# Rewriting a selective-scan vision block: states on partitions, products shared between VectorE and GpSimd, image stages laid between the scans

## The chip, the cores and the metric

The kernel runs on one core of a Trainium2 chip. The metric is the device time of one execution in microseconds, the median of several runs. Every time below is from the profile of one execution of the kernel before, or from its three timed runs. PE stands for TensorE, DVE for VectorE, ACT for ScalarE, POOL for GpSimd, SP for SyncE.

## What is computed

Input x is four images of 64 x 64 pixels with 96 channels in f32. Layer 0 normalizes x by groups and uses only its sign:

```
xz   = s_in * (sign(gn(x)) @ sign(W_in - mean).T) + b_in   # 96 -> 384, halves xp and z
t    = conv3x3(sign(xp + move0), csc * sign(conv_W))       # 192 -> 192
u    = silu(prelu(t + bias) + rp_b1 + xp)                  # [192, 4096] per image
for k in 4 scans:   # rows, columns, rows backwards, columns backwards
    B, C [16, 4096] and 6 further rows = sign products of u's flat data
    delta = softplus(sign product of the signs of those 6 rows + dt_bias)  # [192, 4096]
    h[d,n,l] = exp(delta[d,l] * A[d,n]) * h[d,n,l-1] + delta[d,l] * u[d,l] * B[n,l]
    y[d,l]   = sum_n h[d,n,l] * C[n,l] + D[d] * u[d,l]
y    = layernorm_channels(y of the 4 scans, turned back and added)
x1   = x + s_out * (sign(y * silu(z)) @ sign(W_out).T) + b_out
```

Layer 1 is an attention without softmax over the 4096 tokens (so q (k^T v) is a product with one 96 x 96 matrix per image), and then a feed-forward 96 -> 384 -> 96 whose factors are rounded to 8-bit floats and whose sums are rounded to 16 bits, each behind a layer norm and added to its input.

The bulk is the recurrence: 4 images x 4 scans x 192 channels x 16 states x 4096 steps.

## The kernel before

**Tiling.** Two images form a pair. The pair's 2 x 192 channels fill three tiles of 128 partitions (T = 0, 1, 2). A scan instruction runs along the free axis over 1024 steps of one state n of 128 channels, so there are 2 pairs x 3 tiles x 4 scans x 4 chunks x 16 states = 1536 scan instructions of 128 x 1024.

**Stages of a pair, one after the other** (`layer0_pair`): signs of the normalized x (L248 to L259), in-projection (L276, L277), convolution as 18 products for each 512 pixels (L297, L300) with the activation chain L308 to L319, projections to B, C and the 6 rows (L350 to L376), the scans, and then layer norm, gate and out-projection (L522 to L566). Layer 1 (`layer1`) follows after both pairs. Nothing of one pair's image stages runs beside the other pair's scans.

**The scans' inner loop**, once per state n (`nm` numbers the tiles):

```python
bp = spread("bp", n)              # L474: PE copies row n of B to all 128 partitions, in PSUM
cp = spread("cp", NS + n)         # the same for C
dA = sw.tile([128, CH], F32, name=f"dA_{nm}", tag="dA")
nc.scalar.activation(dA, delta[:, cols], AF.Exp, scale=c["an"][:, KIND[T], k, n : n + 1])
dB = sw.tile([128, CH], F32, name=f"dB_{nm}", tag="dB", bufs=3)
nc.vector.tensor_tensor(dB, du, bp, ALU.mult)
h = sw.tile([128, CH], F32, name=f"h_{nm}", tag="h")
nc.vector.tensor_tensor_scan(h, dA, dB, 0.0 if ci == 0 else carry[:, n : n + 1], ALU.mult, ALU.add)
if ci < NCH - 1:
    nc.gpsimd.tensor_copy(carry[:, n : n + 1], h[:, CH - 1 : CH])
nc.vector.tensor_tensor(dB, h, cp, ALU.mult)
for j in range(2):
    nc.tensor.matmul(
        y[:, 512 * j : 512 * j + 512], ident, dB[:, 512 * j : 512 * j + 512],
        start=(n == 0), stop=(n == NS - 1),
    )
```

In the profile these are L486 (the decay `dA` on ACT), L488 (`dB`), L490 (the scan), L494 (the carry on POOL), L495 (times C) and L497 (PE sums over n by a product with the identity, into `yp`). VectorE has three passes over 128 x 1024 for each of the 1536 pieces. `prepare` (L414 to L431) makes `delta` for the next job in the middle of a job. The order on each engine is that of the program; a tile framework adds the waits.

Of the kernel before, what the change touches and what calls it, by code (L numbers as in the profile page):

```python
# [1 line left out]

# [24 lines left out]
HID = 384  # L27

# Columns of the per-channel parameters.
# [4 lines left out]
# The 192 inner channels of a pair of images fill three tiles of 128 partitions:  # L34
#   0: channels 0..127 of the first image     1: the same of the second
#   2: channels 128..191 of the first on partitions 0..63, of the second on 64..127
# A parameter column comes in two kinds, for tiles 0 and 1 and for tile 2.
KIND = (0, 0, 1)
# [3 lines left out]
def hybrid_kernel(ctx: ExitStack, tc: tile.TileContext, a: dict, out: bass.AP):  # L42
    nc = tc.nc
    const = ctx.enter_context(tc.tile_pool(name="const", bufs=1))
    dram = ctx.enter_context(tc.tile_pool(name="dram", bufs=1, space=DRAM))
# [4 lines left out]
    def load(name, shape, src=None):  # L50
        t = ctile(name, shape)
        nc.sync.dma_start(t, a[name] if src is None else src)
        return t

    # ------------------------------------------------------------------ constants
    ident = ctile("ident", [128, 128])
    make_identity(nc, ident)
    identb = ctile("identb", [128, 128], BF16)
    nc.vector.tensor_copy(identb, ident)
    ones1 = ctile("ones1", [128, 1])  # L60
# [3 lines left out]
    grp = load("grp", [DM, DM])  # L64
    lnm = load("lnm", [128, 6, 128])
    hmask = load("hmask", [DM, DM])

    pv = load("pv", [128, 2, NPV])
    an = load("al", [128, 2, NK, NS])
    nc.scalar.activation(an, an, AF.Exp)  # L70
    nc.vector.tensor_scalar(an, an, -1.0, None, ALU.mult)
    cbias = ctile("cbias", [128, 2])
    nc.vector.tensor_tensor(cbias, pv[:, :, CONV_B], pv[:, :, RP0], ALU.add)
    dbias = ctile("dbias", [128, 2, NK])
    nc.vector.tensor_tensor(dbias, pv[:, :, BD : BD + NK], pv[:, :, DTB : DTB + NK], ALU.add)
    dsum = ctile("dsum", [128, 2])
    nc.vector.tensor_reduce(dsum, pv[:, :, DSK : DSK + NK], AX.X, ALU.add)

    winT = ctile("winT", [DM, 2 * DN], BF16)
    woutT = ctile("woutT", [128, 2, DM], BF16)  # L80
    cw0 = ctile("cw0", [128, 9, DN], BF16)
    cw1 = ctile("cw1", [128, 9, DN], BF16)
    csc = ctile("csc", [128, 2])
    wlT_bc = ctile("wlT_bc", [64, 3, 128], BF16)
    wlT_dt = ctile("wlT_dt", [64, 3, 128], BF16)
    selw = ctile("selw", [99, 128], BF16)
    sld = ctile("sld", [128, 2])
    wdz = ctile("wdz", [48, NK, 8, DN], BF16)
    so_bc = ctile("so_bc", [128, DM])
    nc.sync.dma_start(so_bc, a["s_out"].partition_broadcast(128))  # L90
    bo_bc = ctile("bo_bc", [128, DM])
    nc.sync.dma_start(bo_bc, a["b_out"].partition_broadcast(128))
    rbs = [ctile(f"rb{i}", [99, CH], BF16) for i in range(4)]
    for t in rbs:
        nc.vector.memset(t[96:99, :], 1.0)

    x1d = dram.tile([NB, L, DM], F32, name="x1d", tag="x1d")
    sgd = dram.tile([NB, NK, NR * L], BF16, name="sgd", tag="sgd")

    # ------------------------------------------------------------------ weights  # L100
    with tc.tile_pool(name="prep", bufs=1) as prep, tc.tile_pool(
        name="prep_ps", bufs=2, space=PSUM
    ) as pps:

        def negmean(name, src, n):
            m = prep.tile([src.shape[0]] + list(src.shape[1:-1]) + ([1] if len(src.shape) == 2 else []), F32, name=name)
            nc.vector.tensor_reduce(m, src, AX.X, ALU.add)
            nc.vector.tensor_scalar(m, m, -1.0 / n, None, ALU.mult)
            return m

        def transposed(dst, src):
            """dst[j, i] = src[i, j], for signs"""
            p, f = src.shape
            ps = pps.tile([128, 128], BF16, name="tps", tag="tps")
            nc.tensor.transpose(ps[:f, :p], src, identb[:p, :p])
            nc.vector.tensor_copy(dst, ps[:f, :p])

        wi = prep.tile([128, 3, DM], F32, name="wi")
        nc.sync.dma_start(wi, a["w_in"].rearrange("(t p) j -> p t j", p=128))
        wim = negmean("wim", wi, DM)  # L120
        wis = prep.tile([128, 3, DM], BF16, name="wis")
        for t in range(3):
            nc.scalar.activation(wis[:, t, :], wi[:, t, :], AF.Sign, bias=wim[:, t : t + 1])
            transposed(winT[:, 128 * t : 128 * t + 128], wis[:, t, :])

        wo = prep.tile([DM, DN], F32, name="wo")
        nc.sync.dma_start(wo, a["w_out"])
        wom = negmean("wom", wo, DN)
        wos = prep.tile([DM, 2, 128], BF16, name="wos")
        nc.scalar.activation(wos[:, 0, :], wo[:, 0:128], AF.Sign, bias=wom)  # L130
        for j in range(2):
            nc.scalar.activation(wos[:, 1, 64 * j : 64 * j + 64], wo[:, 128:192], AF.Sign, bias=wom)
        for j in range(2):
            transposed(woutT[:, j, :], wos[:, j, :])

        for j, dst in ((0, cw0), (1, cw1)):
            cwf = prep.tile([128, 9, DN], F32, name="cwf", tag="cwf", bufs=2)
            nc.sync.dma_start(cwf, a["cw_t"][:, j])
            nc.scalar.activation(dst, cwf, AF.Sign)
            cwn = prep.tile([128, 9 * DN], F32, name="cwn", tag="cwn", bufs=2)  # L140
            nc.sync.dma_start(cwn, a["cw_n"][:, j])
            nc.vector.tensor_reduce(csc[:, j : j + 1], cwn, AX.X, ALU.add, apply_absolute_value=True)
        nc.vector.tensor_scalar(csc, csc, 1.0 / (9 * DN), None, ALU.mult)

        wl = prep.tile([128, DN], F32, name="wl")
        nc.sync.dma_start(wl, a["wl_bc"])
        wld = prep.tile([128, DN], F32, name="wld")
        nc.vector.memset(wld, 0.0)
        nc.vector.memset(sld, 0.0)
        for k in range(NK):  # L150
            nc.sync.dma_start(wld[32 * k : 32 * k + NR, :], a["wl_dt"][k])
            nc.sync.dma_start(sld[32 * k : 32 * k + NR, :], a["sl_dt"][k])
        for src, dst, nm in ((wl, wlT_bc, "b"), (wld, wlT_dt, "d")):
            m = negmean("wlm" + nm, src, DN)
            s = prep.tile([128, DN], BF16, name="wls" + nm)
            nc.scalar.activation(s, src, AF.Sign, bias=m)
            for j in range(3):
                transposed(dst[:, j, :], s[:, 64 * j : 64 * j + 64])

        # B and C rows are sl * (an integer of at most 8 bits) + bl.  One bf16 product  # L160
        # copies such a row to all partitions without loss: sl and bl in three bf16
        # parts each, the integers three times and three rows of ones.
        def parts(name, src):
            got = []
            rest = src
            for j in range(3):
                p = prep.tile(list(src.shape), BF16, name=f"{name}p{j}")
                nc.vector.tensor_copy(p, rest)
                got.append(p)
                if j < 2:  # L170
                    r = prep.tile(list(src.shape), F32, name=f"{name}r{j}")
                    nc.vector.tensor_tensor(r, rest, p, ALU.subtract)
                    rest = r
            return got

        slr = prep.tile([96, NK], F32, name="slr")
        nc.sync.dma_start(slr, a["sl_bc"])
        blr = prep.tile([1, 128], F32, name="blr")
        nc.sync.dma_start(blr, a["bl_bc"])
        for j, p in enumerate(parts("sl", slr)):  # L180
            rows = slice(32 * j, 32 * j + 32)
            pf = prep.tile([96, NK], F32, name=f"slf{j}")
            nc.vector.tensor_copy(pf, p)
            for k in range(NK):
                nc.vector.tensor_scalar(
                    selw[rows, 32 * k : 32 * k + 32], ident[rows, rows], pf[rows, k : k + 1], None, ALU.mult
                )
        for j, p in enumerate(parts("bl", blr)):
            nc.sync.dma_start(selw[96 + j : 97 + j, :], p)

        # wdz[(s, c), k, s', d] = sign of Wd[k, d, c] for s == s', 0 elsewhere
        for j, (d0, dn) in enumerate(((0, 128), (128, 64))):
            wd = prep.tile([dn, NK, NR], F32, name=f"wd{j}")
# [585 lines left out]
```

## Time and profile before

| what | value |
|---|---|
| time, median of 3 runs | 9687.55 us (9681.52 to 9706.05) |
| span of the profiled execution | 9661.7 us |
| VectorE busy | 8266.2 us |
| PE busy | 6867.1 us |
| ScalarE busy | 3015.5 us |
| GpSimd busy | 526.9 us |
| PE's mean granted clock | 0.865 |

A row of the groups gives the line, engine, operation, output and input tiles, shapes, count, then busy time and mean length in ns of one, then the idle time in front of them and the instruction that ended it. The slices cut the span into 40 equal parts of 241.5 us and give the busy share in tenths. In the timeline a row begins with the start and the length in us. In the windows each engine has its busy time within a stretch and, in brackets, how many instructions; then come the granted PE clock as a share of full speed, the DMA engines' busy share and the rate moved.

### The profile page before, as it was taken

What the parts mean: (1) busy time and instruction counts of PE and PEld (TensorE: products, weight loads), DVE (VectorE), ACT (ScalarE), POOL (GpSimd) and SP (SyncE); (2) the same over time, 40 slices, a digit from 0 to 9 for tenths busy, and PEclk for the clock granted to TensorE, in tenths of its full rate; (3) what the DMA queues carried; (4) which work ended last, traced back from release to release, by engine and by line L of the source; (5) the groups of instructions that cost most, each with busy time, mean ns of one, the idle gap of its engine ahead of it and who ended that gap; (6) DMA issues with size and microseconds to landing.
All of it is one profiled execution on the core that took longest, in us unless ns stands there. A gap on an engine that the chain in (4) does not pass through costs nothing.

```text
span 9661.7 us, 55915 instructions
## 1 busy us (share of the span) xinstructions
PE 6867.1 (71%) x20931; PEld 2540.6 (26%) x20931; DVE 8266.2 (86%) x6014; ACT 3015.5 (31%) x2906; POOL 526.9 (5%) x1266
## 2 busy tenths in 40 slices
PE   8976666666676776767897666666666677676766
PEld 2232222222222222222324222222222222222244
DVE  2159999999999999998314999999999999999967
ACT  3143333333333333322314333333333333332223
POOL 0000000000000000000000000000000000000012
PEclk6589999999888989999558999998999899999976
DMA  1000000000000000000100000000000000000011
GB/s 39 7 7 3 3 3 4 3 3 3 3 3 3 4 5 5 5 5 15 29 9 7 3 3 3 3 3 3 3 3 3 3 4 5 5 6 7 12 43 27
DMA packets 110605, 73.14 MB, mean 8 GB/s; under 512 B 95076, under 2 KB 95774, under 8 KB 110238
## 3 DMA queue, kind: packets, MB, share of 16 engines
q1 hardware_dynamic: 110334, 69.58, 2.9%
q8 instruction: 164, 2.69, 0.1%
q14 instruction: 107, 0.88, 0.0%
HBM read 24.71 MB, written 13.37 MB: 4 GB/s over the span
## 4 chain that ended last, share of the span: by engine, by line
DVE 58%; PE 22%; issue 16%; ACT 2%; DMA 1%; SPq 0%; POOL 0%; DVEq 0%; POOLq 0%; ACTq 0%
DVE h L490 32%; DVE dB L488 16%; PE yp L497 8%; DVE dB L495 5%; PE cvps L297 3%; PE cvps L300 3%; DVE y L510 1%; PE bp L474 1%; DVE sd L541 1%; PE mu L522 1%; PE tp L350 1%; PE bc L359 1%; PE dt L364 1%; ACT xr L353 1%; PE at L674 0%
## 5 line engine op out<-in xcount | busy, mean ns | idle before, releaser
L497 PE MATMUL yp<-dB,ident 128*128 128x512 f32 x6144 | 3511.3, 700 | 1404.9 <-DVE dB L495 1401.3
L486 ACT ACTIVATE dA<-delta,al 128x1024 f32<-128x1024 f32 x1536 | 1762.8, 1148 | 4794.9 <-DVE h L490 4752.9
L490 DVE TENSOR_TENSOR_SCAN h<-dA,carry,dB 128x1024 f32<-128x1024 f32 x1152 | 2702.0, 2345 | 37.0 <-DVE dB L488 1.9
L497 PEld LDWEIGHTS yp<-dB,ident 128*128 128x128 f32 x6144 | 1170.5, 211 | 3055.9 <-DVE dB L495 1866.4
L488 DVE TENSOR_TENSOR dB<-du,bp 128x1024 f32<-128x1024 f32 x1536 | 1845.5, 1202 | 140.1 <-PE bp L474 139.2
L495 DVE TENSOR_TENSOR dB<-h,cp 128x1024 f32<-128x1024 f32 x1536 | 1862.0, 1212 | 13.3 <-PE cp L474 3.9
L474 PE MATMUL bp<-rb,selw 99*128 99x512 bf16 (+1 forms) x4096 | 1021.2, 412 | 908.9 <-DVE dB L488 885.0
L474 PEld LDWEIGHTS <-selw 99*128 99x128 bf16 (+1 forms) x8192 | 638.7, 109 | 2683.7 <-issue 2493.2
L474 PE MATMUL cp<-rb,selw 99*128 99x512 bf16 (+1 forms) x4096 | 997.3, 404 | 28.3 <-DVE dB L488 16.5
L490 DVE TENSOR_TENSOR_SCAN h<-dA,dB 128x1024 f32<-128x1024 f32 x384 | 876.9, 2284 | 11.0
L494 POOL COPY carry<-h 128x1 f32<-128x1 f32 x1152 | 406.1, 353 | 8208.9 <-DVE h L490 8208.7
L312 DVE TENSOR_SCALAR t<-t,pv 128x512 f32<-128x512 f32 x48 | 23.3, 486 | 610.5 <-ACT t L308 610.5
L297 PE MATMUL cvps<-tp,cw 128*128 128x512 bf16 (+1 forms) x576 | 358.1, 622 | 2.5 <-ACT u L276 2.5
L300 PE MATMUL cvps<-tp,cw 64*128 64x512 bf16 (+1 forms) x576 | 356.4, 619 | 0.0
L427 ACT ACTIVATE sp<-dps,dbias,pv 128x1024 f32<-128x1024 f32 x96 | 115.5, 1203 | 486.3 <-PE dps L414 285.6
L355 DVE COPY xr<-tp 64x1536 bf16<-64x1536 bf16 x64 | 60.8, 950 | 232.0 <-PE tp L350 232.0
L431 DVE TENSOR_TENSOR delta<-sp,sr 128x1024 f32<-128x1024 f32 x96 | 183.3, 1909 | 46.5 <-ACT sp L430 46.5
L308 ACT ACTIVATE t<-cvps,cbias,csc 128x512 f32<-128x512 f32 x48 | 37.3, 777 | 443.4 <-PE cvps L300 443.4
L350 PE MATMUL tp<-identb,xg 128*64 128x128 bf16 x1536 | 157.5, 259 | 15.1 <-DMA xg<-sg 13.2
L541 DVE RECIPROCAL sd<-sd 128x512 f32<-128x512 f32 x48 | 158.6, 3332 | 10.6 <-ACT sd L540 8.4
L522 PE MATMUL mu<-y,lnm 128*128 128x512 f32 x224 | 130.0, 721 | 45.7 <-DVE yc L532 44.6
L350 PEld LDWEIGHTS <-xg 128*64 128x64 bf16 x1536 | 138.3, 160 | 70.9 <-issue 70.9
(181 smaller groups left out, 3702.9 us busy)
## 6 DMA issues: line engine op xcount, KB each, us to landing
rb<-ibc SPq DMA_DIRECT2D x384, 64.0 KB
xt<-in_x SPq DMA_DIRECT2D x16, 384.0 KB
xr<-in_x SPq DMA_DIRECT2D x32, 192.0 KB
x1d<-o SPq DMA_DIRECT2D x32, 192.0 KB
x<-x1d SPq DMA_DIRECT2D x16, 384.0 KB
out<-o SPq DMA_DIRECT2D x32, 192.0 KB
xg<-sg SPq DMA_DIRECT2D x16, 172.0 KB
cwf<-in_cw_t SPq DMA_DIRECT2D x2, 864.0 KB
```

What stands on the lines that cost most here:

```text
L297: nc.tensor.matmul(ps[prow, :], c["cw0"][:, t, co], tpad[j][:, win[0], win[1]], start=(t == 0), stop=False)
L300: nc.tensor.matmul(ps[prow, :], c["cw1"][rows, t, co], tpad[2][rows, win[0], win[1]], start=False, stop=(t == 8),)
L350: nc.tensor.transpose(tp[:, j // 6, 128 * (j % 6) : 128 * (j % 6) + 128], src, identb)
L474: nc.tensor.matmul(ps[rows, 512 * h : 512 * h + 512], w.to_broadcast([99, rows.stop - rows.start]), t[:, 512 * h : 512 * h + 512], start=True,
L486: nc.scalar.activation(dA, delta[:, cols], AF.Exp, scale=c["an"][:, KIND[T], k, n : n + 1])
L488: nc.vector.tensor_tensor(dB, du, bp, ALU.mult)
L490: nc.vector.tensor_tensor_scan(h, dA, dB, 0.0 if ci == 0 else carry[:, n : n + 1], ALU.mult, ALU.add)
L494: nc.gpsimd.tensor_copy(carry[:, n : n + 1], h[:, CH - 1 : CH])
L495: nc.vector.tensor_tensor(dB, h, cp, ALU.mult)
L497: nc.tensor.matmul(y[:, 512 * j : 512 * j + 512], ident, dB[:, 512 * j : 512 * j + 512], start=(n == 0), stop=(n == NS - 1),)
L522: nc.tensor.matmul(ps, c["lnm"][:, m, :], src[s], start=(i == 0), stop=(i == len(terms[T]) - 1))
L541: nc.vector.reciprocal(sd, sd)
```

## The change

The kernel is rewritten around the same arithmetic. Six things are new.

1. **A piece** is 32 channels x 4 states on 128 partitions, 1024 steps: again 1536 pieces, each with one scan. B and C are stored in DRAM and loaded spread over the 32 channels; delta and delta times u are stored and loaded spread over the 4 states. The sum over 4 states is a PE product with a 0/1 matrix (`sum4`) that adds four partitions, accumulated over four pieces.
2. **Shares.** GpSimd makes the injected product of every piece (`inject`). The product by C goes to VectorE or to GpSimd by a tally of assumed costs, kept while the program is built (`Tally`, `scan`). The decay is written to PSUM.
3. **Order.** One loop over all 1536 pieces (`Scans.run`) writes the order by hand: injected products four pieces ahead, the decay one ahead, the sum over states three behind, stores some rounds after their producers. In each round one step of the image stages of other images is taken (`next(back, None)`): the prologue of images 1 to 3 and the epilogue of images 0 to 2 stand between scans, and most of the last image's norm. Only image 0's prologue (head) and the last image's end (tail) stand alone.
4. **u also stored turned**: beside `ud` (rows) there is `utd` (columns), so that the column scans load whole rows. Their outputs are turned back in a stage of its own (`turn`).
5. **Sign products on the whole array or in bf16**: the projections and delta's products use 128 rows or columns of the array, signs are in 8-bit floats, delta's weights are padded with zeros; u's projection chain is in bf16.
6. **Head and tail**: where an image stands alone, VectorE takes a part of ScalarE's work in the convolution (`v`), the norm and the feed-forward, and in the tail two more lanes work on blocks of 512 pixels side by side. All activations come from one table set (silu, softplus and roots by Exp and Ln).

The core of the diff:

```diff
-                    bp = spread("bp", n)
-                    cp = spread("cp", NS + n)
...
-                    nc.scalar.activation(dA, delta[:, cols], AF.Exp, scale=c["an"][:, KIND[T], k, n : n + 1])
...
-                    nc.vector.tensor_tensor(dB, du, bp, ALU.mult)
...
-                    nc.vector.tensor_tensor(dB, h, cp, ALU.mult)
...
+    def load_bc(self, w, to, b, e, ci, q):
+        c = self.c
+        t = c.p.bc.tile([128, CH], F32, name=f"bc{w}_{b}_{e}_{ci}_{q}", tag=f"bc{w}")
+        src = c.bcd[b][KORD[e], 16 * w + 4 * q : 16 * w + 4 * q + 4, CH * ci : CH * ci + CH]
+        c.nc.sync.dma_start(t, src.unsqueeze(0).to_broadcast([32, 4, CH]))
+        to[b, e, ci, q] = t
...
+            src = c.dld[KORD[e]][b][w, 32 * g : 32 * g + 32, CH * ci : CH * ci + CH]
+            c.nc.sync.dma_start(t, src.unsqueeze(1).to_broadcast([32, 4, CH]))
...
+    def decay(self, i):
...
+        t = c.p.dA.tile([128, CH], F32, name=f"dA_{i}", tag="dA")
+        c.nc.scalar.activation(t, self.dlt[i // NQ][0], AF.Exp, scale=c.anm[:, g, NQ * KORD[e] + q : NQ * KORD[e] + q + 1])
...
+    def inject(self, i):
...
+        t = c.p.w.tile([128, CH], F32, name=f"w_{i}", tag="w")
+        c.gps.tensor_tensor(t, self.dlt[i // NQ][1], self.bt[b, e, ci, q], ALU.mult)
...
+        lead = c.vec.us - c.gps.us
+        c.vec.us, c.gps.us = max(0.0, min(lead, 8.0)), max(0.0, min(-lead, 8.0))
+        pool = c.vec.us + 1.2 > c.gps.us + 2.4
+        dA, w, cr = self.dAs[i], self.ins[i], self.ct[b, e, ci, q]
+        h = c.p.h.tile([128, CH], F32, name=f"h_{i}", tag="h") if pool else dA
+        c.vec.tensor_tensor_scan(h, dA, w, first, ALU.mult, ALU.add)
+        (c.gps if pool else c.vec).tensor_tensor(w, h, cr, ALU.mult)
...
+        for x in range(4):
+            c.nc.tensor.matmul(
+                y[32 * x : 32 * x + 32, g % 2, :], c.sum4, prod[:, 256 * x : 256 * x + 256],
+                start=(q == 0), stop=(q == NQ - 1), tile_position=(0, 32 * x),
+            )
...
+        for i in range(n):
+            self.at = i
+            self.loads(i)
+            if i >= 1:
+                self.carry(i - 1)
+            if i + 1 < n:
+                self.decay(i + 1)
+            full = i % 8 == 3 and i > 8
+            if full:
+                self.evacuate(i - 4)
+            elif i >= 3:
+                self.reduce(i - 3)
+            if i + AHEAD < n:
+                self.inject(i + AHEAD)
+            self.scan(i)
+            c.later.tick()
...
+            interleave(lanes)
+            next(back, None)
```

`c.vec` and `c.gps` are VectorE and GpSimd with the tally; `prepare` in `lanes` makes delta for the chunk after next, one part for every eight pieces; `carry` copies the last column of h on ScalarE.

## The prediction

> **What bounds the kernel now.** I read the page first (busy shares, slices, groups), then the timeline of 12 us inside the scans, then the windows by stage. The page says which engine is full and with what:
>
> ```profile
> span 9661.7 us, 55915 instructions
> PE 6867.1 (71%) x20931; PEld 2540.6 (26%) x20931; DVE 8266.2 (86%) x6014; ACT 3015.5 (31%) x2906; POOL 526.9 (5%) x1266
> ...
> DVE  2159999999999999998314999999999999999967
> ...
> L486 ACT ACTIVATE dA<-delta,al 128x1024 f32<-128x1024 f32 x1536 | 1762.8, 1148 | 4794.9 <-DVE h L490 4752.9
> L490 DVE TENSOR_TENSOR_SCAN h<-dA,carry,dB 128x1024 f32<-128x1024 f32 x1152 | 2702.0, 2345 | 37.0 <-DVE dB L488 1.9
> L488 DVE TENSOR_TENSOR dB<-du,bp 128x1024 f32<-128x1024 f32 x1536 | 1845.5, 1202 | 140.1 <-PE bp L474 139.2
> L495 DVE TENSOR_TENSOR dB<-h,cp 128x1024 f32<-128x1024 f32 x1536 | 1862.0, 1212 | 13.3 <-PE cp L474 3.9
> ```
>
> VectorE is at 9 tenths wherever there are scans, hardly waits (37, 140 and 13 us), and ScalarE waits 4753 us for it. GpSimd does 5%. The timeline, VectorE alone (start, length, instruction), gives the pace:
>
> ```profile
> 3001.20 2.34 DVE L490 TENSOR_TENSOR_SCAN h<-dA,carry,dB 128x1024 f32<-128x1024 f32 x1
> 3003.46 1.19 DVE L488 TENSOR_TENSOR dB<-du,bp 128x1024 f32<-128x1024 f32 x1
> 3004.57 1.21 DVE L495 TENSOR_TENSOR dB<-h,cp 128x1024 f32<-128x1024 f32 x1
> 3005.70 2.34 DVE L490 TENSOR_TENSOR_SCAN h<-dA,carry,dB 128x1024 f32<-128x1024 f32 x1
> ```
>
> From start to start: 2.26 for the scan, 1.11 and 1.13 for the products, 4.50 us a piece; 1536 pieces make 6912 us. The windows (length, busy time of PE, PEld, DVE, ACT and POOL, clock, DMA share, GB/s) show that the rest is image work with VectorE idle, and what DMA can do:
>
> ```profile
> 0.00:483.00 483.00, 423.62 (x1211) 136.81 (x1212) 93.25 (x233) 120.68 (x174) 14.41 (x11) 0.62 0.08 23
> ...
> 900.00:2700.00 1800.00, 1226.99 (x2942) 433.88 (x2942) 1751.99 (x1153) 568.49 (x498) 93.82 (x265) 0.91 0.01 3
> ...
> 100.00:330.00 230.00, 227.46 (x419) 45.83 (x418) 36.68 (x57) 46.61 (x72) 0.00 (x0) 0.50 0.03 9
> ...
> 10.00:15.00 5.00, 0.24 (x1) 0.09 (x1) 1.38 (x3) 1.64 (x1) 0.00 (x0) 1.00 0.99 406
> ```
>
> The first pair of images takes 483 us before its first scan (230 us of it PE alone, the convolution at a granted clock of 0.50); the second pair some 530 more, in which no scan runs. In the scans VectorE works 1752 of 1800 us.
>
> **What the Trainium skill says.** (1) "GPSIMD Engine Reference", section 3.1: a product of two f32 inputs of 2048 elements takes 4497 ns there, about twice VectorE's. The trace of before has no two-input operation on GpSimd; its one-input cast of 512 elements has a median of 668 ns, which agrees with twice that for two inputs. (2) "SBUF — State Buffer", section "Who interferes with whom": a VectorE instruction with two SBUF inputs excludes a GpSimd instruction that reads SBUF; one with a single SBUF input does not. Nothing in before shows it, since GpSimd is idle. (3) "ScalarE: Activation LUTs", "What ACT_TABLE_LOAD costs": an activation without pointer operands takes 186 ns + 0.833 ns per element; with the 93 ns that the section gives for one pointer, 1024 elements come to 1132 ns, and the trace has 1148.
>
> **The change, part by part.**
>
> *The piece.* There are again 1536 scans of 128x1024, now 32 channels by 4 states. Of VectorE's three passes the first (u times delta times B) goes to GpSimd for every piece, and the last (times C) is shared out by a tally as the program is built: counting the program's instructions, 905 stay on VectorE and 631 go to GpSimd. B, C, delta and delta times u no longer come from PE; DMA loads them spread over partitions. The decay exp(delta A) is written to PSUM, so that a scan has one SBUF input (the injected product) and a product by C one (C) where VectorE makes it; by (2) these leave GpSimd free.
>
> *VectorE in the scan stage.* 1536 scans x 2.26 = 3471 us. 905 products x 1.13 = 1023. Preparing delta: 192 parts x 2 operations of 512; such rows of before take 663 and 678 ns, 0.60 by the overlap of 0.08 to 0.1 seen above: 230. Convolution of three images: 48 x 3 x 0.62 = 89. Norm, attention and feed-forward that stand between scans: 28 norm blocks with 4 operations of 512 and 24 feed-forward blocks with 2, 160 x 0.6 = 96, and 28 small ones at 0.25 = 7. Sum 4916 us.
>
> *GpSimd.* 1536 + 631 = 2167 products of 1024. The halved price is 2.25 us; the start-up is not halved, so up to 2.35; I take 2.3: 4984 us. From below: 2.1 us if the second input costs less than the first.
>
> So two engines end up nearly equal, at 3.20 and 3.24 us a piece. Neither hides the other: the tally alternates between both, four injected pieces ahead is all the slack.
>
> *ScalarE.* 1536 decays x 1.15 = 1766; 1152 carry copies at the price of (3), 0.19 = 219; 192 evacuations at 0.59 (row of the 128x512 cast) = 113; 960 operations of delta and about 1700 of the image stages, of 512 elements, at 0.68 (rows of before lie between 0.59 and 0.81) = 1810. Together 3.9 ms, 3.7 of them beside the scans: 70% of the stage. It is hidden on the mean, but it is in order: carry copy i-1 waits for scan i-1, and behind it stand decay i+1 and all image work.
>
> *PE.* The sum over states is four f32 products of 256 columns a piece. In before's timeline four of 512 columns take 1.98 us; half of that is 1.0 us a piece, 1.5 ms in all. Image stages add 1.0 to 1.7 ms by clock. Hidden: 50 to 62%.
>
> *DMA.* 1280 spread loads of 512 KiB = 671 MB. In 5.2 ms that is 129 GB/s, against 406 in the window above. u stored turned makes the loads of the column scans whole rows; its stores are in 128-byte pieces, 6144 a store, 12 beside scans. With the 384-byte rows of x1d moving at 261 GB/s in before (1.5 MB, 4096 pieces, 6 us) such a store takes about 9 us, and the loads are issued 13 to 17 us ahead. I cost it at nothing.
>
> *Head.* Only image 0 stands before the scans, and of its sign projections only two scans of four. Load, sums, turning: 27 us; in-projection 32 activations x 0.75 = 24; convolution 288 products at the 0.54 us from start to start that the clock of 0.50 gives in before = 156, with 16 more of the recomputed projection 165, the last part's chain 12; projection of two scans a quarter of the pair's 153 us window, 40, plus its stores and loads through DRAM 25; first delta parts and spread loads 17. VectorE's share of the convolution lies under PE and costs nothing. Sum 310 us.
>
> *Tail.* Of the 32 norm blocks (8 an image) 28 stand beside scans in the program's order; 4 of the last image are left, and its 8 feed-forward blocks. By the chain of a block's operations at the rows above, a norm block takes some 28 us and a feed-forward block 20. Two rounds of three lanes at 28 us, 8 us for the last y to go through DRAM, 9 for the small matrices; three rounds of 20 us and 3 us of store. Sum 136 us. VectorE's share shortens ScalarE's queue there; the round is a chain, so I take no more from it.
>
> *Sum.* The scan stage has 4984 us of work on its fuller engine. In before VectorE idles 2.7% of its scan stage with every other engine at 70% or less; here two engines are full and two more at 60 to 70% in order, so I take double, 5.3%: 5248. With 310 and 136: **5694 us**.
>
> **Rivals.** *In-order ScalarE and PE set the pace* (6250 us). The convolution's steps put six products (1.5 to 3.3 us) and up to three activations (2 us) plus a delta step (1.4 us) into one piece's time; decay and carry behind them come late, with about 1.9 us of slack. If half of the pieces took 4.3 us (a convolution step of 3.3 us and the sum's 1.0 on PE) and the others 3.24: 1536 x 3.78 = 5800, + 446. For it: the ScalarE share, the 0.50 clock; against: means of 70 and 62%. *GpSimd is quicker than priced* (5500): 2.1 us leaves VectorE the bound, 4916 + 3% + 446. *DMA sets the pace* (6550): 671 MB at 110 GB/s; the same lines are read 32 or 4 times; against: 406 GB/s. *The two engines exclude each other* (10346, slower than before): if the scan counts as two SBUF inputs by its carry, 4984 + 4916 + 446. For it: 1152 scans do read a carry from SBUF beside the product; against: (2) speaks of tensors, and the carry is one element.
>
> **How the numbers follow.** Main case 0.55, ScalarE and PE 0.25, GpSimd quicker 0.12, DMA 0.05, exclusion 0.03. Range: below, VectorE's 4916 without a stall and a head and tail of 420: 5330. Above, the ScalarE and PE case with 6% of stalls more: 6350. Outside stand DMA, exclusion and edges of the others, 0.15 to 0.2. Only exclusion ends above 9687: faster 0.96, same 0.01, slower 0.03.
>
> **What would show it.** Right: the page has GpSimd and VectorE both above 85%; the group of injected products has a mean of 2.2 to 2.4 us, the scans 2.3; VectorE's slices are at 8 or 9 from the third to the last but one; from start to start of a scan 3.2 to 3.5 us; the first scan starts near 310, the last ends near 136 before the end. Wrong: injected products or scans far longer than these (exclusion); waits of VectorE on the decay of several hundred us (ScalarE); waits on spread loads (DMA); a head of 400 us and more, if the convolution in 8-bit runs slower than 0.54 us a product or if the one-byte strided sign writes, like the 1608 ns of before's strided sign row, hold ScalarE.

## The result and the profile after

The changed kernel takes 5776.87 us (median of 4 runs, 5769.06 to 5794.46), against 9696.8 us for the kernel before, run beside it: a ratio of 0.596, 95% interval 0.5946 to 0.5973. Forecast were 5694 us, within 5330 to 6350.

The page of the kernel after, with the lines that answer to those of before:

```profile
span 5775.5 us, 61921 instructions
PE 3419.4 (59%) x19813; PEld 1339.9 (23%) x19813; DVE 5176.7 (90%) x3422; ACT 3672.1 (64%) x5620; POOL 5080.7 (88%) x2291
...
DVE  3299999999889999999999999999999999999984
...
POOL 2099999999889999999998999999999999999980
...
L386 POOL TENSOR_TENSOR w<-dl,bc 128x1024 f32<-128x1024 f32 x1536 | 3578.4, 2354 | 149.2 <-PE yp L1264 73.8
L1223 ACT ACTIVATE dA<-dl,anm 128x1024 f32<-128x1024 f32 x1536 | 1714.0, 1116 | 494.6 <-DVE w L386 254.6
...
L386 DVE TENSOR_TENSOR_SCAN dA<-dA,cy,w 128x1024 f32<-128x1024 f32 x680 | 1593.1, 2343 | 109.7 <-ACT dA L1223 94.0
L386 POOL TENSOR_TENSOR w<-h,bc 128x1024 f32<-128x1024 f32 x631 | 1483.8, 2352 | 191.6 <-DVE h L386 181.0
L386 DVE TENSOR_TENSOR w<-dA,bc 128x1024 f32<-128x1024 f32 x905 | 1108.6, 1225 | 57.9 <-DVE dA L386 0.9
...
L575 ACT ACTIVATE sg<-cz 96x512 fp8e5<-96x512 f32 x64 | 159.0, 2484 | 22.1 <-DVE cz L386 22.0
```

GpSimd went from 5% to 88%, VectorE from 86% to 90%, and both are at 8 or 9 tenths from the third slice to the last but one. A scan is as long as before (2343 ns against 2345) with GpSimd at work beside it. One row is out of line with its size: the signs `sg` (the output of Sign on ScalarE, one byte each) at 2484 ns for 512 elements.

The windows (length, then PE, PEld, which is PE's loading of weights, DVE, ACT, POOL, granted clock, DMA share, GB/s) cut the span at the first scan and at the end of the last:

```profile
0.00:288.00 288.00, 153.43 (x715) 88.13 (x716) 75.09 (x136) 150.17 (x198) 43.66 (x106) 0.75 0.41 89
288.00:5610.00 5322.00, 3156.90 (x18742) 1202.56 (x18741) 5026.65 (x3152) 3456.04 (x5310) 5023.65 (x2178) 0.67 0.61 193
5610.00:5776.00 166.00, 109.10 (x356) 49.26 (x356) 75.00 (x136) 65.87 (x112) 13.43 (x9) 0.72 0.33 89
```

Head 288, scan stage 5322, tail 166; forecast were 310, 5248 and 136. In the scan stage each of the two engines works 94.4% of the time, their sums alike to 3 us.

The timeline of VectorE and GpSimd inside the stage (start, length, instruction):

```profile
2500.82 2.35 DVE L386 TENSOR_TENSOR_SCAN dA<-dA,cy,w 128x1024 f32<-128x1024 f32 x1
2501.98 4.66 POOL L386 TENSOR_TENSOR w<-dl,bc 128x1024 f32<-128x1024 f32 x2
2503.20 1.23 DVE L386 TENSOR_TENSOR w<-dA,bc 128x1024 f32<-128x1024 f32 x1
...
2505.86 2.34 DVE L386 TENSOR_TENSOR_SCAN h<-dA,cy,w 128x1024 f32<-128x1024 f32 x1
...
2508.12 2.33 DVE L386 TENSOR_TENSOR_SCAN dA<-dA,cy,w 128x1024 f32<-128x1024 f32 x1
2508.28 2.35 POOL L386 TENSOR_TENSOR w<-h,bc 128x1024 f32<-128x1024 f32 x1 [1.64 <-DVE h L386]
```

From a scan to the scan behind it 2.26 us go by, as before. From a scan to the product of its own output it is 2.38, since that product needs the scan's end. Scans with their own product behind them also write PSUM here, where the others write SBUF, but that isn't the reason: in the run with the decay in SBUF (below) the own product still starts 0.03 us after the scan's end, any other instruction 0.08 us before it (medians, and in the kernel after the same). At the last line GpSimd has stood 1.64 us for a scan.

### The profile page after: what moved, and what is told of

It is laid out like the page before. It is cut to its first block, busy times and chain, and to the rows that moved or that the text cites. A ratio compares the mean times of both kernels' runs of the same rounds, so it can differ in the third digit from the quotient of the medians.

```text
span 5775.5 us, 61921 instructions
## 1 busy us (share of the span) xinstructions
PE 3419.4 (59%) x19813; PEld 1339.9 (23%) x19813; DVE 5176.7 (90%) x3422; ACT 3672.1 (64%) x5620; POOL 5080.7 (88%) x2291
## 5 line engine op out<-in xcount | busy, mean ns | idle before, releaser
L386 POOL TENSOR_TENSOR w<-dl,bc 128x1024 f32<-128x1024 f32 x1536 | 3578.4, 2354 | 149.2 <-PE yp L1264 73.8
L1223 ACT ACTIVATE dA<-dl,anm 128x1024 f32<-128x1024 f32 x1536 | 1714.0, 1116 | 494.6 <-DVE w L386 254.6
L1264 PE MATMUL yp<-w,sum 128*32 128x256 f32 x12288 | 1323.3, 547 | 845.8 <-ACT ys L1276 447.7
L386 DVE TENSOR_TENSOR_SCAN dA<-dA,cy,w 128x1024 f32<-128x1024 f32 x680 | 1593.1, 2343 | 109.7 <-ACT dA L1223 94.0
L386 POOL TENSOR_TENSOR w<-h,bc 128x1024 f32<-128x1024 f32 x631 | 1483.8, 2352 | 191.6 <-DVE h L386 181.0
L386 DVE TENSOR_TENSOR w<-dA,bc 128x1024 f32<-128x1024 f32 x905 | 1108.6, 1225 | 57.9 <-DVE dA L386 0.9
L386 DVE TENSOR_TENSOR_SCAN h<-dA,cy,w 128x1024 f32<-128x1024 f32 x472 | 1103.8, 2340 | 12.0 <-ACT dA L1223 10.2
L1264 PEld LDWEIGHTS yp<-w,sum 128*32 128x32 f32 x12288 | 363.1, 137 | 1941.0 <-issue 836.8
L386 DVE TENSOR_TENSOR_SCAN dA<-dA,w 128x1024 f32<-128x1024 f32 x225 | 513.6, 2283 | 38.3 <-ACT dA L1223 29.9
L562 PE MATMUL cv<-tp,cw 96*96 96x512 fp8e5 x1152 | 390.8, 499 | 137.5 <-ACT r L611 110.0
L386 DVE TENSOR_TENSOR_SCAN h<-dA,w 128x1024 f32<-128x1024 f32 x159 | 362.3, 2279 | 32.0 <-POOL w L386 23.7
L575 ACT ACTIVATE sg<-cz 96x512 fp8e5<-96x512 f32 x64 | 159.0, 2484 | 22.1 <-DVE cz L386 22.0
```

The source lines that it names most:

```text
L386: return getattr(self.eng, name)(out, *args, **kw)
L562: nc.tensor.matmul(ps, c.cw[:, j, t, 96 * h : 96 * h + 96], tpad[j][:, 8 * q + dy : 8 * q + dy + 8, dx : dx + IW], start=(j == 0 and t == ...
L575: nc.scalar.activation(sg.bitcast(F8).rearrange("p (h e i) -> p h i e", h=8, e=2), pz.rearrange("p (h i e) -> p h i e", h=8, e=2), AF.Sign ...
L1223: c.nc.scalar.activation(t, self.dlt[i // NQ][0], AF.Exp, scale=c.anm[:, g, NQ * KORD[e] + q : NQ * KORD[e] + q + 1])
L1264: c.nc.tensor.matmul(y[32 * x : 32 * x + 32, g % 2, :], c.sum4, prod[:, 256 * x : 256 * x + 256], start=(q == 0), stop=(q == NQ - 1), tile ...
```

## The experiments

Twelve kernels, each a small edit of the kernel after. Ratios are to the kernel before.

**The two shared engines.** All products by C on one of them, first VectorE:

```diff
-        pool = c.vec.us + 1.2 > c.gps.us + 2.4
+        pool = False
```

> Every product by C stays on VectorE (1536 instead of 905). Shared-work theory (VectorE and GpSimd together are the bound of the scan stage): VectorE gets 631 x 1.15 = 726 us on top of its 5027 busy us there, GpSimd falls to 1536 x 2.33 = 3579; scan stage about 5830, time about 6280 us, VectorE at 97% or more of the scan stage. Rival (ScalarE and PE in order set the pace): VectorE has 295 us of idle time to fill and the time rises by less than that, to 5780 to 6000.

6400.39 us, ratio 0.6604 (0.6594 to 0.6613). Then GpSimd (`pool = True`):

> All 1536 products by C go to GpSimd, none to VectorE. Theory of the prediction (the fuller of the two engines sets the pace, 2.33 us a product on GpSimd from start to start): 3072 x 2.33 = 7158 us of products, with 288 + 166 for head and tail and 1 to 3% of waits 7680 to 7830; VectorE falls by about 1100 us. Rival (something other than the two engines holds the stage, such as PE, ScalarE or transfers): clearly under 7600 or above 7900.

7561.19 us, ratio 0.7799 (0.7789 to 0.781). The scan stages in the windows, VectorE full in the first and GpSimd in the second:

```profile
286.00:6236.00 5950.00, 3212.75 (x18782) 1226.77 (x18781) 5789.24 (x3784) 3528.30 (x5313) 3581.73 (x1552) 0.64 0.55 173
```

```profile
286.00:7386.00 7100.00, 3450.26 (x18742) 1232.18 (x18741) 4048.51 (x2247) 3463.30 (x5310) 7088.25 (x3083) 0.59 0.46 145
```

VectorE alone full works 97.3% of its stage, GpSimd alone full 99.8%. The second time lies under the 7600 named there as the rival's, yet not for the rival's reason: nothing but GpSimd holds that stage. A product there starts every 2.31 us (not 2.33), 3072 x 2.31 = 7096 us of a stage of 7100, without the 1 to 3% of waits expected. So the fuller engine sets the pace. With both full, in the kernel after, each is idle for 5.6% of the stage; for whom they wait is read further down. The first run came 120 us above its expectation, in good part because 631 more products follow their own scan at 2.38 instead of 2.26 (631 x 0.12 = 76 us).

**Is the decay in PSUM what lets them run together?** The decay goes to SBUF; to make room, products are injected three pieces ahead and two buffers are given up. A control has the same without the move:

```diff
-AHEAD = 4
+AHEAD = 3
...
-        t = c.p.dA.tile([128, CH], F32, name=f"dA_{i}", tag="dA")
+        t = c.p.dS.tile([128, CH], F32, name=f"dA_{i}", tag="dS")
```

> The decay goes to SBUF instead of PSUM, so a scan has two SBUF inputs, and so has a product by C on VectorE (to make room: three injected products ahead instead of four, 8 and 7 buffers instead of 9 and 8; e5 has the same without the SBUF decay and is the one to compare with). If two SBUF inputs exclude a GpSimd instruction that reads SBUF: 2167 x 2.33 + 1536 x 2.26 + 905 x 1.15 = 9560 us in turn, time about 10000 us, slower than the kernel before, with scans or GpSimd's products far longer than 2.35 us in the profile or idle between them. If they do not exclude each other: as e5, within 1%.

> Three injected products ahead instead of four, with 8 buffers for them instead of 9, and 7 scratch buffers of 512 instead of 8. Shared-work theory: less slack between the two full engines, so more handover waits: 5800 to 5950 us. ScalarE and PE theory: their lateness, not the slack of GpSimd, counts: within 0.3% of 5777.

Decay in SBUF: 9527.94 us, ratio 0.9831 (0.9812 to 0.9851). Control: 5818.02, ratio 0.6004 (0.5994 to 0.6014). The instructions on the tile `dA` with the decay in SBUF (count, then min/median/max in ns):

```profile
L386 DVE TENSOR_TENSOR w<-dA,bc x905: 1225/3130/3210, 308.9 to 9331.1; 128x1024 f32<-128x1024 f32 x181
...
L386 DVE TENSOR_TENSOR_SCAN dA<-dA,cy,w x680: 2316/4362/4464, 434.1 to 9328.7; 128x1024 f32<-128x1024 f32 x170
```

and GpSimd's products on its page:

```profile
L386 POOL TENSOR_TENSOR w<-dl,bc 128x1024 f32<-128x1024 f32 x1536 | 5804.7, 3801 | 64.7 <-DMA dl<-dld 60.9
L386 POOL TENSOR_TENSOR w<-h,bc 128x1024 f32<-128x1024 f32 x631 | 2506.7, 3973 | 773.0 <-DVE h L386 734.6
```

The shortest are as short as ever (1225 and 2316 ns), the medians longer by 1.9 and 2.0 us, most of one GpSimd product (2.35), and GpSimd's own products by 1.4 to 1.6: for most of their length a scan or product on VectorE and a product on GpSimd no longer run side by side. For some of it they do, so the time is under the 10000 us expected, and the kernel is not slower than the one before but level with it. This is what the Trainium skill says ("SBUF — State Buffer", section "Who interferes with whom": a VectorE instruction with two SBUF inputs contends with a GpSimd instruction that reads SBUF), and in the kernel after, with one input in PSUM, nothing of it is seen: 2343, 1225 and 2354 ns. The carry, which 1152 scans of the kernel after read from SBUF beside the product, doesn't act as a second input: they take 2340 to 2343 ns, the 384 without it 2279 to 2283. Against its control the tile's place is worth 3710 us, nearly as much as the whole rewrite gains (3920).

**More slack.** Five pieces ahead instead of four, with one buffer more for products, one less for images and B's loads one piece earlier:

```diff
-AHEAD = 4
+AHEAD = 5
```

> Five injected products ahead instead of four, 10 buffers (scratch 7 instead of 8, and B's loads for the next chunk one piece earlier). Shared-work theory: GpSimd's 181 us of waiting for a scan in front of its products by C shrink, VectorE follows only in part: 5690 to 5760 us. ScalarE and PE theory: within 0.3% of 5777.

5770.41 us, ratio 0.5955 (0.5946 to 0.5963): as after, above the whole range of the shared-work theory and where the other theory had it. GpSimd's wait for scans fell only from 181 to 162 us. So slack in front of VectorE is not what is missing at four pieces; at three (the control above, with two buffers less) it is, by 41 us, and there it was the shared-work theory that held. What VectorE waits for is asked next.

**Who is late in the scan stage?** VectorE's largest waits from 288 to 5610 us (total, times, longest):

```profile
DVE dA L386 <- ACT dA L1223: 123.9, 82, 8.5
DVE u L386 <- ACT e L586: 44.3, 28, 3.4
...
DVE h L386 <- ACT dA L1223: 17.9, 18, 2.5
```

and GpSimd's:

```profile
POOL w L386 <- DVE h L386: 181.0, 174, 6.0
POOL w L386 <- PE yp L1264: 74.3, 33, 5.9
POOL g L631 <- DMA utd<-ut: 14.4, 2, 9.6
```

VectorE waits for decays (142 us in 100 places) and only 30 us for GpSimd's products; GpSimd waits for VectorE. A further 32 us of VectorE's idle time are no wait for another engine: 905 times 0.035 us between a scan and its own product. With all products on VectorE, the same ScalarE work makes it wait only 26 us for decays, so lateness depends on how tight the pace is. ScalarE's timeline before one of the longest waits (scan at 3096.11, 8.4 us late):

```profile
3082.22 1.12 ACT L1223 ACTIVATE dA<-dl,anm 128x1024 f32<-128x1024 f32 x1
3094.35 0.58 ACT L889 COPY ysum<-ys 96x512 f32<-96x512 f32 x1 [11.01 <-PE ys L836]
3094.83 0.16 ACT L1254 COPY cy<-dA 128x1 f32<-128x1 f32 x1
3094.89 1.12 ACT L1223 ACTIVATE dA<-dl,anm 128x1024 f32<-128x1024 f32 x1
```

It is not at work there but stands 11 us for PE's image products; the carry and the decay are queued behind. PE in turn had stood 12.41 us for the load of `ey` from `yd`, and the next sum over states stands behind it in PE's queue (GpSimd waits 74 us for such sums in the whole stage). So a late load of an image stage reaches the scan over two engines in order. 19 of the 100 waits are over 1.5 us; they make up 65 of the 142.

ScalarE's longest image operation is the sign; two runs make it short. One writes the signs in the order of the computation; the projection then reads other values in each place:

```diff
-                                sg.bitcast(F8).rearrange("p (h e i) -> p h i e", h=8, e=2),
-                                pz.rearrange("p (h i e) -> p h i e", h=8, e=2), AF.Sign, saturate=False,
+                                sg.bitcast(F8), pz, AF.Sign, saturate=False,
```

> The one-byte signs are written in the order in which they are computed, not strided into pairs; the sign data then have their pixels in another order, so the projection to delta, B and C takes other values. An activation of 96x512 should fall from 2.48 us towards 0.6, ScalarE by some 120 us in all. Theory (two shared engines set the pace, ScalarE only through single late decays): head -15 (8 signs by 1.9 us), scan stage 0 to -40, time 5720 to 5762. Rival (ScalarE sets the pace): scan stage -100 or more, time 5660 or less.

5718.57 us, ratio 0.59 (0.5892 to 0.5908): 1 us under the theory's range, far from the rival's. The other keeps every sign in its place and changes the order in which the activation goes through them:

```diff
-                                sg.bitcast(F8).rearrange("p (h e i) -> p h i e", h=8, e=2),
-                                pz.rearrange("p (h i e) -> p h i e", h=8, e=2), AF.Sign, saturate=False,
+                                sg.bitcast(F8).rearrange("p (h e i) -> p h e i", h=8, e=2),
+                                pz.rearrange("p (h e i) -> p h e i", h=8, e=2), AF.Sign, saturate=False,
```

> The same signs go to the same places, but the activation runs through its elements in the order of the output: it reads f32 from PSUM at a stride of two elements and writes runs of 32 bytes. Theory (the strided one-byte write is what costs 2.48 us): the activation falls below 1.0 us, first scan near 264, scan stage -35, time 5710 to 5728 as with the contiguous signs. Rival (a strided side costs whichever it is): the activation stays above 2 us and the time at 5777.

5728.03 us, ratio 0.5906 (0.5897 to 0.5915), at the theory's upper edge. The signs in this run:

```profile
L575 ACT ACTIVATE sg<-cz x64: 573/593/594, 91.6 to 2683.4; 96x512 fp8e5<-96x512 f32 x64
```

2486 ns at the median became 593, with the read now at a stride of two f32 and the 512 bytes written one after the other. So it was the write: in the kernel after, each byte lies 31 or 32 bytes from the one before it. The Trainium skill says in "SBUF — State Buffer", section "Door 1: The DMA port swizzle", that "consecutive accesses to the same 16-byte line hit full bandwidth" and that crossing to a new line costs; the direction agrees. In the second run the first scan comes at 261.8 (26 us earlier) and the stage takes 5294 us (28 less), though ScalarE has 82 us less to do in it. So a third of what ScalarE is spared in the stage comes out at the end; as the pace it would have given all of it. Nor are the decays less late (151 us against 142). What falls is VectorE's wait for `u`, from 44 to 20 us: the sign stands ahead of `e`, `u` waits for `e`, and a scan stands behind `u`.

**What the turned u costs.** Neither the copies nor the stores of `utd` are made, and column scans read u in row order:

```diff
-                            if pq % 4 == 0:
+                            if False:
...
-        ud = (c.utd if k % 2 else c.ud)[b].rearrange("h p (n l) -> (h p) n l", l=IW)
+        ud = c.ud[b].rearrange("h p (n l) -> (h p) n l", l=IW)
```

> The turned copy of u is neither made nor stored; the column scans read u in row order, so the column scans compute with another u. This takes away 48 stores of 128-byte pieces and their ScalarE copies, and leaves every load and every operation of the scans. Theory of the prediction (stores hidden on the DMA queues, ScalarE with slack): within 0.3% of after, 5760 to 5794. Rival (DMA or ScalarE sets the pace of the scan stage): 5727 or less.

5740.73 us, ratio 0.5923 (0.5915 to 0.5931): 36 us, between the two expectations. 14 of it is in the head (first scan at 274.3), 23 in the stage; there the copies alone are 53 us of ScalarE's work, and what the copies and what the stores cost isn't parted. One wait of ScalarE in the kernel after's head, from 205 to 288 us, says how the stores cost time:

```profile
ACT xr L644 <- DMA utd<-ut: 10.1, 1, 10.1
```

The projection's first tile `xr` doesn't read `utd`. By the code it comes from a pool that is opened when the pool of `ut` has been closed; so it waits for the store to leave `ut` (that they share memory is read from the code, not from the trace). GpSimd's 14.4 us above, by the same reading, are this wait in the stage. What the turned copy saves in the loads of column scans wasn't tried.

**VectorE's share in head and tail**, both given back to ScalarE:

```diff
-    e.alone = True
...
-                    if alone:
+                    if False:
```

> VectorE's share of the convolution in the head and of norm and feed-forward in the tail goes back to ScalarE; nothing else changes. Theory of the prediction (the share lies under PE in the head, and a tail round is a chain, so the share is worth nothing): first scan at 288 +- 10 us, tail 166 + 0 to 15, time 5777 to 5795. Rival (ScalarE is the pace of head and tail: in the head's convolution it is busy 98 of 150 us already with the share given away): first scan 12 us or more later, tail 20 to 40 us longer, time 5810 to 5830.

5826.47 us, ratio 0.6007 (0.5999 to 0.6015). The window of its tail:

```profile
5601.00:5825.00 224.00, 166.89 (x488) 73.48 (x484) 24.55 (x41) 100.94 (x176) 4.70 (x6) 0.78 0.25 66
```

Neither theory holds: the tail is 58 us longer than after's 166, PE with 488 products instead of 356 (where VectorE and GpSimd don't add the scans' y, PE does it by f32 products) and ScalarE 35 us busier; how much each adds isn't parted. But the first scan comes at 273.8, 14 us *earlier*. (The time falls in the rival's range only because both of its parts are off, in opposite ways.) With only the head's share given back (the last line of the diff):

> Only VectorE's share of the head's convolution goes back to ScalarE; the tail's share stays. Theory (the share lengthens the chain from the products to their release, as the run without both shares shows by a first scan at 274): first scan at 274 +- 2, tail 166, time 5757 to 5770. Rival (a first scan that comes earlier is lost again in the scan stage): 5772 or more.

5761.8 us, ratio 0.5941 (0.5932 to 0.595), first scan at 273.6: as the theory had it, but for a tail of 172 us. (In the profiles of runs that leave the tail alone it takes 166 to 174 us, so 7 us there say nothing.) The share slows the head. The timeline there, one part of 512 pixels in the kernel after:

```profile
129.85 0.77 ACT L611 ACTIVATE r<-cv,cbias,csc 96x512 f32<-96x512 f32 x1 [1.61 <-DVE v L608]
...
130.67 5.75 PE L562 MATMUL cv<-tp,cw 96*96 96x512 fp8e5 x18 [1.55 <-ACT r L611]
...
131.56 2.45 ACT L575 ACTIVATE sg<-cz 96x512 fp8e5<-96x512 f32 x1 [0.94 <-DVE cz L386]
133.52 0.92 ACT L583 ACTIVATE e<-cz 96x512 f32<-96x512 f32 x1
...
134.47 0.63 ACT L585 ACTIVATE e<-e 96x512 f32<-96x512 f32 x1
135.13 0.63 ACT L586 ACTIVATE e<-e 96x512 f32<-96x512 f32 x1
135.85 0.69 DVE L386 TENSOR_TENSOR u<-cz,e 96x512 f32<-96x512 f32 x1 [4.32 <-ACT e L586]
...
136.47 0.81 DVE L608 TENSOR_SCALAR v<-cv,acs,acb 96x512 f32<-96x512 f32 x1
...
137.31 0.77 ACT L611 ACTIVATE r<-cv,cbias,csc 96x512 f32<-96x512 f32 x1 [1.55 <-DVE v L608]
```

Read from `r` to `r`: r to sg 1.71, sg to e 1.96, then 0.95, 0.66, to u 0.72, to v 0.62, to r 0.84; together 7.46 us a part. Each link starts as the one before it ends, or shortly before that on the same engine. The moved `v` stands behind `u` in VectorE's queue, `u` waits for the last `e`, and `r` starts only when `v` has ended; PE waits at the end of this loop. Five of the 15 steps from `r` to `r` take longer, 8.5 to 9.1 us; in all they take 118. The last two runs cut into it. First two PSUM tiles for PE's parts instead of two halves of one:

```diff
-            two = c.p.dA.tile([128, CH], F32, name=f"cv2_{b}", tag="dA") if alone else None
+            two = [c.p.dA.tile([128, CH], F32, name=f"cv{x}_{b}", tag="dA") for x in range(2)] if alone else None
...
-                    ps = (two[:, at : at + 512] if alone else bank("cv" + nm, 0))[0:96]
+                    ps = (two[n % 2][:, 0:512] if alone else bank("cv" + nm, 0))[0:96]
```

> In the head the convolution's parts go in turn to two PSUM tiles instead of two halves of one. In the trace of after each part's 18 products start only when the part before has been read (1.55 us behind ScalarE's r, 16 parts). Theory (the two halves count as one buffer): that wait goes, first scan at 262 to 273, time 5750 to 5765. Rival (the wait is another one, or PE's clock falls by what the wait gave it): first scan 283 or later, time 5770 or more.

5769.44 us, ratio 0.5951 (0.5943 to 0.596), first scan at 281.0: between the two. From 85 to 215 us PE's wait for `r` falls from 32.3 to 10.7 us, and a wait of 13.3 us for `u` at `cz` takes its place. A buffer more for PE takes away the long steps (all 15 are now 7.4 to 7.8 us, 112 in all) but helps no further while the loop through ScalarE and VectorE sets the pace. Why PE waits for `r` at all with two tiles stays open.

All three together, signs in output order, `v` on ScalarE and two tiles:

> Signs in output order, the head's share back on ScalarE and two tiles for the head's convolution, together. Where PE is left as the head's only chain (16 parts of 18 products at 4.1 to 5.75 us and one of 0.4): first scan at 240 to 256; scan stage 5287 and tail 166 as with contiguous signs: 5690 to 5712. Rival (the three remove the same wait): first scan at 262 to 265, 5715 to 5720.

5698.55 us (5696.5 to 5711.15), ratio 0.588 (0.587 to 0.589): 78 us under the kernel after. The loop in its head:

```profile
126.15 0.76 ACT L611 ACTIVATE r<-cv,cbias,csc 96x512 f32<-96x512 f32 x1
...
126.96 4.08 PE L562 MATMUL cv<-tp,cw 96*96 96x512 fp8e5 x18 [0.18 <-ACT r L611]
...
127.92 0.59 ACT L575 ACTIVATE sg<-cz 96x512 fp8e5<-96x512 f32 x1 [1.01 <-DVE cz L386]
...
130.22 0.76 ACT L610 ACTIVATE v<-cv,acb,acs 96x512 f32<-96x512 f32 x1
...
130.89 0.76 ACT L611 ACTIVATE r<-cv,cbias,csc 96x512 f32<-96x512 f32 x1
```

4.74 us from r to r instead of 7.46; the 15 steps take 71 us instead of 118, and the first scan comes 50 us earlier, at 237.5 (expected 240 to 256). `u` no longer stands in the loop, and PE, which hardly waits (0.18 us), is close to its pace. In the scan stage (5299 us) it gains 23. One by one the three gained 49, 15 and 7 us, so they don't remove the same wait.

## Why the prediction was right, and where its steps failed

**The bound: right.** Two engines at 94.4% of the stage, a piece every 5322 / 1536 = 3.46 us (3.2 to 3.5 forecast), and the fuller engine sets the pace when all products are on one of them.

**GpSimd's price: right.** Taken at 2.3, measured at 2.31 where it never waits; the Trainium skill's "GPSIMD Engine Reference", section 3.1, halved as an estimate, gave 2.25 (the page measured an addition, not a product). The cast, at twice 668 ns for 512 elements, would have given 2.67 for 1024, so it agreed less well than the prediction says. 2167 x 2.31 = 5006 us against 4984.

**VectorE's work: 111 us low** (5027 against 4916). With each instruction counted up to the start of the next, the scans make 3530 us (3471 forecast), the products by C 1037 (1023) and the 711 others 459 (422, at 0.6 or less; they take 0.65). The scan's price of 2.26 is that of one before another instruction: 905 have their own product behind them, which keeps VectorE busy until their end, 2.34 with a carry; the 384 scans without a carry are shorter and take some of this back.

**The handover, 5.3%: near, in part by luck.** 5322 against 5024 of work is 5.9%; doubling the 2.7% of before was a guess. That one full engine loses 2.7% (VectorE) or 0.2% (GpSimd), and two lose more, is what the two one-sided runs show. But the two don't lose it to each other alone: VectorE's largest waits are for ScalarE, as "two more at 60 to 70% in order" allowed. Of these, 44 us for `u` are shown to be half the slow signs' doing; the 142 us for late decays stand, traced to ScalarE waiting in order in the cases looked at, but no run removed them.

**The head: 288 against 310, right only in sum.** The convolution starts at 83 us; "load, sums, turning: 27" and 24 for the in-projection had it at 51. The 24 held (60 to 83 us), the 27 became 60. In ScalarE's own queue there are only issues of loads up to 31 us, of `anm` last:

```profile
12.18 18.24 ACTq L245 DMA_DIRECT2D anm<-in_al  x23
```

(23 of 24; the view ends at 30 us.) The first activation that prepares weights stands behind them, and PE waits 31.8 us for it; no run moved these issues. The convolution takes 131 us (83 to 214) against 177: 18 products take 5.75 us in the part shown, not 18 x 0.54 = 9.7, and PE isn't the pace, though the prediction took it to be; the loop over ScalarE and VectorE is. From there to the first scan it is 74, against 82. And "VectorE's share of the convolution lies under PE and costs nothing" failed: it costs 14 us.

**The turned copy at nothing: failed, by 36 us** for copies and stores together. The prediction asked only whether the transfer fits beside the scans; in the head ScalarE waits 10 us for such a store, ahead of work that doesn't read it. How the 23 us in the stage divide stays open.

**The tail: 166 against 136.** The failed term is "8 us for the last y to go through DRAM". In the chain of waits the last scan, over at 5609.7, is followed by

```profile
5619.26 9.52 DMA ln1b<-yd
5628.87 10.94 DMA eu<-ud
5641.97 3.73 PE mu L836 x4
```

so that the third lane starts 32 us behind the scan instead of 8, which is 24 of the 30 us. Each lane's loads are issued after those of the lane before, and from 5620 to 5645 us they move at 262 GB/s; whether their order or their amount is the reason wasn't tried. VectorE's and GpSimd's share in the tail, from which the forecast took nothing, is worth 58 us.

**The rivals.** ScalarE and PE as the pace: refuted at its size; ScalarE is busy 65% of the stage (70% forecast), and taking 82 us from it gave 28. The strided sign writes, which the prediction named as a sign of being wrong, did hold ScalarE: 2.49 us for what it had priced at 0.68, 49 us of the time. DMA: refuted as pace; it moves 193 GB/s in the stage, 1066 MB in all and not only the 671 of spread loads, and GpSimd waits 4 us for such loads there. Exclusion: its mechanism is real, its condition not met; with the decay in SBUF it gives 9528 us, less than the 10346 forecast, since the engines still overlap in places. The range's upper end doesn't come out of its own working: 5800 with 6% more, and 446, make 6594 and not 6350. The tail, 30 us, and the stage, 74, less 22 in the head, make up the 82 us between forecast and profile.

## What to carry to other kernels

When two engines share one kind of work, ask first whether they can run side by side with the operands where they are: here the memory of one operand decided 3710 us. Two engines balanced to the same load lost 5.6% of the stage each, where one full engine lost 0.2 to 2.7%, and part of it to a third engine that worked in order. An operation moved to an idle engine can cost time if it gets in line behind an instruction that waits for the engine it left: follow the queue from one repetition to the next before counting it as hidden.

## What was not expected of the hardware

- A one-byte activation output whose neighbours in time lie 32 bytes apart took 2486 ns for 512 elements; with the bytes one after the other 593. The f32 read from PSUM at a stride of two elements cost nothing that shows (593 against 592 with both sides in order, medians).
- A scan costs 0.12 us more from start to start when the next VectorE instruction reads its output (2.38 against 2.26).
